# Two graph layers on one NeuronCore: first-layer sums one turn behind their messages, no shared PSUM banks, whole pair buffers in the second layer, and SyncE register loads without an assert

## The chip, the core and the metric

The kernel runs on one core of one Trainium2 chip. The metric is the device time of one execution in microseconds (us). Engines are written as the profile writes them: PE is TensorE (PEld its weight loads), DVE VectorE, ACT ScalarE, POOL GpSimd, SP SyncE (SPq is its queue of DMA issues). PEclk is the clock that TensorE was granted, in tenths of full speed.

## What is computed

There are 6,250 nodes with 512 features and 100,000 edges, sorted by destination. Destinations are drawn as the square of a uniform number, so low-numbered nodes have more incoming edges.

```python
def gat(feat, dist, src, dst, W, b, w_src, w_dst):          # layer 0
    h = leaky_relu(feat @ W.T + b, 0.2).reshape(N, 8, 64)
    e = leaky_relu((h * w_src).sum(-1)[src] + (h * w_dst).sum(-1)[dst], 0.2)
    m = segment_max(e, dst)
    ex = exp(e - m[dst])
    s = segment_sum(ex, dst)
    msg = h[src] * (ex / s[dst] * dist)[:, :, None]
    return segment_sum(msg, dst).reshape(N, 512)

def sage(x, src, dst, deg, W_self, W_neigh, bias, gamma, beta):   # layer 1
    h = x @ W_self.T + (segment_sum(x[src], dst) / deg) @ W_neigh.T + bias
    return layernorm(h) * gamma + beta

x = x + gat(relu(layernorm(x)), edge_attr_8, ...)
x = x + sage(relu(layernorm(x)), ...)
```

All is float32.

## The kernel before

**Streams, windows, turns.** The sorted edge list is cut into four streams q of equal length. Streams 0 and 1 are pair 0, streams 2 and 3 pair 1. Each stream is walked in NW = 66 windows of T = 3 tiles of 128 edges. A window of a stream touches at most 64 destination rows, starting at a base row that is looked up in a table; windows of stream 0 share one base in groups of four, those of stream 1 in groups of two, and streams 2 and 3 change it each window (GRP = (4, 2, 1, 1)). One pass through the loop body is a turn.

**First layer, node part.** The first 265 us hold the layer norm and the dense product of layer 0; the results go to a table `h0_d` in DRAM, each row with the 512 values of h and the 8 of e_src. `ed_d` holds e_dst.

**First edge loop** (about 265 to 1450 us). For each window POOL fetches the h rows of 12 tiles, one indirect DMA each (`gather`, L731), into one of NB = 4 window buffers `gbuf`. `load_edges` has SP fetch the destination rows' e_dst (L766) and the segment penalties (L768). `onehot` (L774, DVE) makes the 0/1 matrices of edge to destination; they are turned over on PE (`front_turn`, L793) and multiplied with e_dst (`front_dst`, L805). `soft_pick` (step ECa, ACT, L822) picks e_src out of the gathered rows and `soft_src` (SSa, PE, L814) adds it to the same bank. Scans on DVE find the maximum of each segment (NX, SCF, SCR), PE turns the result (TE, TM, L860), LM/SUB/EXP/AA make the weights, and the messages are formed in place in `gbuf`: D0c to D1b on DVE (L954, L961), the H steps on ACT (L973). Then the sums: `add_ones` (SV, L998) and the six `add_up` steps A00 to A12 (L990) multiply the one-hot matrices with the messages into one PSUM bank per pair. `finish` (C0, C1) adds the window before, moved to the new base by a selector matrix CS (`carry_sel`), with an f32 matmul (L1007, and L1008 for the weight sums). `evac` (EV0, EV1, L1018) copies the bank to SBUF tile `ws` on ACT; `store` has SP write rows whose base is done. Finished blocks of 128 nodes ("slots") are loaded back by `slot_load`, divided, added to x, normalised and written to `h1_d` by `slot_run`, a generator that ORDER advances at each "S" and "L".

**What sets the order.** Nothing is reordered by a scheduler: the program runs under a manual schedule, so each engine's queue follows the order in which Python calls the steps. ORDER is that list for a turn k; STEPS gives for each name the window it works on, as an offset from k. FT0=(4, …) works on window k+4, A00=(0, …) on window k. `when` drops steps outside 0 to 65. At the end of a turn the twelve gathers of window k+4 are issued; each waits until the sum that last read its part of the buffer is done.

**Shared banks.** `goes_on(k, p)` is true for pair 0 at odd windows, where neither stream 0 nor stream 1 changes its base. There the bank is not evacuated after window k-1 and not carried: the matmuls of window k go on adding to it. In layer 0 this starts at window KR = 9, since up to there the carried sum may have to be rescaled; in layer 1 at window 1.

**Second edge loop** (about 1590 to 2650 us). The same streams and windows without attention: POOL gathers 12 tiles of `h1_d` per turn (`gather1`, L1273) into a ring of five buffers of half a window each; PE sums (L1302); the carry is split in two parts (`carry_split`, L1333 and L1334, DVE) and added with two fp32r matmuls (`finish1`, L1310); ACT evacuates (L1322). In the same turns each finished slot goes through the dense products (L581), the layer norm and the residual. ORDER1 and STEPS1 lay out this turn.

**SP's register loads.** `base` and `slot_load` read a row number from SBUF into a register (L721 and others). In the trace each is a TENSOR_LOAD, a FUSED_REGOPS and a SEQ_ASSERT on SP.

Of the kernel before, what the change touches and what calls it, by code (L numbers as in the profile page):

```python
# [8 lines left out]
FT = mybir.dt.float32  # L9
FR = mybir.dt.float32r  # L10
# [34 lines left out]
def gnn_kernel(ctx, tc, x, srcp, dstp, attrp, wt0, b0, wsrc, wdst, wts, wtn, bias1, gamma1, beta1, out):  # L45
# [3 lines left out]
    order.enter_context(tc.manual_schedule())  # L49

# [144 lines left out]
    btab = con.tile([1, NQ, NW], I32, name="btab")  # L195
# [149 lines left out]
    def i_base():  # L345
        V.tensor_copy(dfr, dstt[0:1, :, 0:NL:T])
        V.tensor_scalar(bmx, bhi[0:1, :], -float(M), 0.0, op0=OP.add, op1=OP.max)
        V.tensor_tensor(out=br, in0=dfr, in1=bmx.unsqueeze(2).to_broadcast([1, NQ, NW]), op=OP.min)
        V.memset(br[:, 0, 0:1], 0.0)
        for q in range(NQ):  # L350
            for i in range(1, GRP[q]):
                n = len(range(i, NW, GRP[q]))
                V.tensor_copy(br[:, q, i::GRP[q]], br[:, q, 0:NW:GRP[q]][:, 0:n])
        V.tensor_copy(btab, br)
        yield
        yield
# [361 lines left out]
    def base(k, q):  # L718
        k -= k % GRP[q]
        if (k, q) not in breg:  # L720
            breg[k, q] = S.value_load(btab[0:1, q, k:k + 1], min_val=0, max_val=N - M)  # L721
        return breg[k, q]
# [11 lines left out]
    def attr_turn(k, h):  # L734

        c, kk = divmod(k, CH)
        if kk == CH - 3 + h // 4 and (k < 0 or (c + 1) * CH < NW):
            c += 1
            nt = min(CH * T, NL - c * CH * T)
            if h == 0:  # L740
                AT[c] = lp.tile([128, H, NQ * CH * T], FT, name="at")
                AT.pop(c - 2, None)
            av = AN[c].rearrange("t (e h) -> t h e", h=H)
            AP_[h] = pv = bank("sf"[(k - 1) % 2])[:, 0:4 * NQ * nt].rearrange("p (h t) -> p h t", h=4)
            for i in range(4):
                P.transpose(pv[:, i], av[0:NQ * nt, h + i], ident[0:NQ * nt, 0:NQ * nt])
            if h:
                AN.pop(c)
# [176 lines left out]
    def fac_rest(k):  # L925
        F9[k] = f9 = lp.tile([128, 2, H + 2], FT, name="f9")
        V.tensor_scalar(f9[:, :, H + 1], FP[k][:, :, H], -1.0, 1.0, op0=OP.mult, op1=OP.add)
# [47 lines left out]
    BANKS = [bank("w", 2) for _ in range(2)]  # L975

    def goes_on(k, p, first=KR):

        return p == 0 and first <= k < NW and k % GRP[0] and k % GRP[1]

    def add_up(k, p, j):
        if j >= njof(k):
            return
        oh, g_ = OHs[k], GT[k]
        if j == 0:
            BK[p] = BANKS[p]
        w = BK[p]
        for q2 in range(2):
            r = slice(64 * q2, 64 * q2 + 64)
            P.matmul(w[r, :], oh[:, p, j, q2], g_[:, 2 * p + q2, j, 0:D], start=(j == 0 and not goes_on(k, p)), stop=False, skip_group_check=True)  # L990
# [10 lines left out]
    def finish(k, p):  # L1001

        w, sv = BK.pop(p), SV[k]
        if k:
            c = WC[k] if k < KR else WS[k - 1]
            if not goes_on(k, p):
                P.matmul(w, CS[k][:, p], c[:, p, 0:D], start=False, stop=True, skip_group_check=True)  # L1007
            P.matmul(sv[:, p], CS[k][:, p], c[:, p, None, D:AW].to_broadcast([128, 2, H + 1]), start=False, stop=True, skip_group_check=True)  # L1008
        BK[k, p] = w
        if p:  # L1010
            GT.pop(k)

    def evac(k, p):
# [3 lines left out]
        if not goes_on(k + 1, p):  # L1017
            A.activation(WS[k][:, p, 0:D], w, AF.Copy)  # L1018
# [10 lines left out]
    def store(k, p, acc, width):  # L1029
        for q2 in range(2):  # L1030
# [8 lines left out]
            if k + 5 < NW:  # L1039
                base(k + 5, q)  # L1040
# [11 lines left out]
    def slot_load(s, r=None):  # L1052
        if r is None:
            r = S.value_load(tab[0:1, s:s + 1], min_val=0, max_val=NP - 128)
# [40 lines left out]
    def none():  # L1095
        return iter(())
# [3 lines left out]
    10 01 00 30 11 20 02 22 12 21 31 32  # L1100
# [4 lines left out]
    for k in range(NB - 1):  # L1105
        gather(k)
# [19 lines left out]
    def slot(w):  # L1126
# [8 lines left out]
        FT0=(4, front_turn, 0), FT0c=(4, front_copy, 0), FT1=(3, front_turn, 1), FT1c=(3, front_copy, 1),  # L1135
        FD=(3, front_dst), ECa=(3, soft_pick, 0), SSa=(3, soft_src, 0), ECb=(2, soft_pick, 1), SSb=(2, soft_src, 1), EZ=(2, soft_copy), SCF=(2, max_before), NX=(2, max_ahead),
# [4 lines left out]
        RESC=(0, later(rescale, KR)), D0c=(0, message_part), D0a=(0, message, 0, 0), D0b=(0, message, 0, 1), D1a=(0, message, 1, 0),  # L1141
        D1b=(0, message, 1, 1),
        SV=(0, add_ones), A00=(0, add_up, 0, 0), A01=(0, add_up, 0, 1), A02=(0, add_up, 0, 2),
        A10=(0, add_up, 1, 0), A11=(0, add_up, 1, 1), A12=(0, add_up, 1, 2), C0=(0, finish, 0), C1=(0, finish, 1),
        EV0=(0, evac0), EV1=(-1, evac1), OH=(4, onehot), CS=(0, later(carry_sel)))
    STEPS.update({f"H{p}{i}": (0, message_act, p, i) for p in range(2) for i in range(4) if p or i})
    ORDER = """
    H13 H01 D0b S D0a D1a TE ECb H11 NX S SCR S FT1 A00 D0c FL EV1 SV S H12 RESC A01 AT0 H03 H02 OH TM A10 S CM FDf A02
    FX S RS S LM RH AT0c CS SSb C0 SUB PF L FT1c S EZ EXP D1b SCF S A11 H10 AT1 ECa AT1c FT0 S AA F9a S A12 F9b S EV0
    FD SSa C1 FT0c S  # L1150
# [9 lines left out]
    for k in range(-4, NW + 1):  # L1160
        sl_ = slot_run(slot(k - 3)) if slot(k - 3) is not None and slot(k - 3) not in LATE else none()
        c, kk = divmod(k, CH)
        when(k + 4, load_edges)
        if slot(k - 2) is not None and slot(k - 2) not in LATE:
            slot_load(slot(k - 2))
# [16 lines left out]
        if k >= -1:  # L1182
            when(k + NB, gather)
# [84 lines left out]
    def gather1(k, p):  # L1268
        GT[k, p] = g_ = ring[:, (2 * k + p) % 5]
        for j in range(njof(k)):  # L1270
            for q2 in (1, 0):
                c = k * T + j
                G.indirect_dma_start(out=g_[:, q2, j, :], out_offset=None, in_=h1_d[0:NT * 128, :],  # L1273
                                     in_offset=bass.IndirectOffsetOnAxis(ap=idx[:, 2 * p + q2, c:c + 1], axis=0))
# [3 lines left out]
    ring = lay1.enter_context(tc.tile_pool(name="gp1", bufs=1)).tile([128, 5, 2, T, D], FT, name="g")  # L1278
    own1 = wp1.tile([128, LATES, D], FT, name="own1")
    small = lay1.enter_context(tc.tile_pool(name="small1", bufs=5))  # L1280
    with tc.tile_pool(name="raw1", bufs=1) as tmp:
# [5 lines left out]
        for n in range(5):  # L1287
            gather1(*divmod(n, 2))
# [6 lines left out]

    def add_up1(k, p, j):
        if j >= njof(k):
            return
        if j == 0 and not goes_on(k, p, 1):
            BK[p] = bank("w", 2) if p else bank("s")  # L1300
        for q2 in range(2):
            P.matmul(BK[p][64 * q2:64 * q2 + 64, :], OHs[k][:, p, j, q2], GT[k, p][:, q2, j, :],  # L1302
                     start=(j == 0 and not goes_on(k, p, 1)),
                     stop=False, skip_group_check=True)

    def finish1(k, p):
        w = BK[p]
        if k and not goes_on(k, p, 1):
# [8 lines left out]
    def evac1_(k, p):  # L1317
        if p == 0:
            WS[k] = lp.tile([128, 2, D], FT, name="ws")
        w = BK.pop((k, p))  # L1320
        if not goes_on(k + 1, p, 1):
            A.activation(WS[k][:, p], w, AF.Copy)  # L1322
# [4 lines left out]
    def carry_split(k, p):  # L1327

        if goes_on(k + 1, p, 1):
            return  # L1330
# [6 lines left out]
    def slot1_load(s, r=None):  # L1337
        if r is None:
            r = S.value_load(tab[0:1, s:s + 1], min_val=0, max_val=NP - 128)
# [9 lines left out]
    def own_load(s):  # L1349
        r = S.value_load(tab[0:1, s:s + 1], min_val=0, max_val=NP - 128)  # L1350
# [116 lines left out]
    PIECES = [ring[:, (2 * NW + i // (2 * T)) % 5, i % (2 * T) // T, i % T] for i in range(NLATE)]  # L1467

    def late_sums(i):
        s = LATE[i]  # L1470
        y = PIECES[i]
# [68 lines left out]
    def early(w, f):  # L1540
        return at(w, f) if slot(w) not in LATE else none()

    STEPS1 = dict(EV0=(0, evac1_, 0), CS0=(-1, carry_split, 0), EV1=(-1, evac1_, 1), CS1=(-1, carry_split, 1), OH=(1, onehot, 3),
                  SEL=(1, carry_sel, FR), C0=(0, finish1, 0), C1=(0, finish1, 1), G0=(3, gather1, 0), G1=(2, gather1, 1))
    STEPS1.update({f"A{p}{j}": (0, add_up1, p, j) for p in range(2) for j in range(T)})
    SLOTS1 = dict(MEAN=(-2, slot1_mean), SUMS=(-1, slot1_sums))
    ORDER1 = """
    en en la MEAN A00 A01 A02 la A10 CS0 C0 EV1 OH en PUT en PRE G1 sl la SEL en en SUMS CS1 sl A11 A12 EV0 G0 C1 sl  # L1550
    """.split()

    last, ends = none(), none()
    for k in range(-1, NW - 1):
# [5 lines left out]
        for name in ORDER1:  # L1560
            if name == "sl":
                step(sl_)
            elif name == "la":
                step(last)
            elif name == "en":
                step(ends)
            elif name == "PUT":
                run(ends)
                put_out()
            elif name == "PRE":  # L1570
                run(pre)
            elif name in SLOTS1:
                d, f = SLOTS1[name]
                early(k + d, f)
            elif k >= 0 or name[0] != "G":
                d, f, *a = STEPS1[name]
                when(k + d, f, *a)
        if 12 <= k < 12 + NLATE:
            late_beta(k - 12)
        last, ends = sl_, last  # L1580
    k = NW - 1
    sl_ = early(k - 2, slot1_run)
    carry_split(k - 1, 0)
# [188 lines left out]
```

## Time and profile before

Three runs took 2757.96, 2762.36 and 2772.39 us, the median being 2762.36.

| | profiled execution |
|---|---|
| its own time | 2755.29 us |
| span in the trace | 2753.4 us |
| mean granted PE clock | 0.866 |
| PE busy | 2154.7 us (78%) |
| POOL busy | 1699.9 us (62%) |
| DVE busy | 1524.9 us (55%) |
| ACT busy | 1106.5 us (40%) |
| gathers, layer 0 | 784, mean 973 ns on POOL |
| gathers, layer 1 | 784, mean 978 ns on POOL |

The 1.9 us between span and time lie outside the traced span. The page divides the span into 40 slices of 69 us. In slices 5 to 21 (the first edge loop) DVE and ACT show 4 to 7 tenths, in slices 24 to 38 (the second) 4 to 5 and 1 to 2, while PE shows 8 in nearly all. A share over the whole span mixes these stages, so the stages are read one by one: by busy times in windows of the span, by what ended each idle time of an engine, and by the chain of waits that ended last.

### The profile page before, as it was taken

The page shows a single profiled execution, that of the slowest core. Times are in us where ns is not written, and L with a number is a line of the kernel's source. Part 1 is how long each engine was busy: PE and PEld are TensorE (multiplying, and loading weights), DVE is VectorE, ACT ScalarE, POOL GpSimd, SP SyncE. Part 2 cuts the span into 40 slices and gives each one's busy share as a digit, 9 for nine tenths or more (in the row PEclk, how much of TensorE's full clock was granted, in tenths as well). Part 3 has the DMA queues.
Part 4 walks back from the last instruction along what each step waited for, and adds up shares of the span by engine and source line. Part 5 has one row for each costly group of instructions (what it writes and reads, how often), then busy time and mean ns, then how long its engine had stood idle before and what let it go on. Part 6 is the DMA issues. An engine that isn't in the chain of part 4 may idle for free.

```text
span 2753.4 us, 34180 instructions
## 1 busy us (share of the span) xinstructions
PE 2154.7 (78%) x8780; PEld 1068.8 (39%) x8780; DVE 1524.9 (55%) x3120; ACT 1106.5 (40%) x3469; POOL 1699.9 (62%) x1675
## 2 busy tenths in 40 slices
PE   7982688888888888888885266787887788878886
PEld 5761233333333333333332033343443444434444
DVE  7874556576667666666667122254544444444446
ACT  6860445566556565555654111122222222222212
POOL 5666466666666666666652666666667666766652
PEclk9995789888888998898987588898898898998898
DMA  6636476777787888877774777788878787878872
GB/s 206 203 114 181 129 205 191 218 239 230 235 246 237 240 236 238 241 237 235 241 221 129 244 214 221 235 250 251 254 240 257 237 258 243 251 248 249 252 238 91
DMA packets 264713, 611.63 MB, mean 222 GB/s; under 512 B 63604, under 2 KB 74372, under 8 KB 264510
## 3 DMA queue, kind: packets, MB, share of 16 engines
q0 software_dynamic: 125440, 414.35, 51.6%
q1 hardware_dynamic: 138494, 193.97, 21.3%
q8 instruction: 72, 1.18, 0.2%
q14 instruction: 131, 1.07, 0.1%
q10 hardware_dynamic: 576, 1.05, 0.1%
HBM read 511.44 MB, written 97.76 MB: 221 GB/s over the span
## 4 chain that ended last, share of the span: by engine, by line
PE 50%; issue 16%; DVE 15%; another core or an unknown queue 9%; ACT 5%; DMA 3%; POOL 1%; SPq 1%; ACTq 0%; POOLq 0%; DVEq 0%
PE ps_w L990 10%; PE ps_b L581 6%; PE ps_s L1302 6%; PE ps_f L581 5%; PE ps_w L1302 5%; DVE gbuf L954 3%; PE ps_z L805 2%; PE ps_w L1007 2%; ACT gbuf L973 2%; PE ps_w L1310 2%; PE ps_t L793 1%; PE ps_w L581 1%; PE ps_s L998 1%; PE ps_z L814 1%
## 5 line engine op out<-in xcount | busy, mean ns | idle before, releaser
L731 POOL DMA_INDIRECT gbuf<-h_d,idx x784 | 762.6, 973 | 461.3 <-issue 197.7
L1273 POOL DMA_INDIRECT g<-h_d,idx x784 | 766.9, 978 | 391.0 <-issue 198.8
L990 PE MATMUL ps_w<-gbuf,oh 128*64 128x512 f32 x1568 | 524.8, 709 | 79.1 <-issue 47.4
L973 ACT ACTIVATE gbuf<-gbuf,aa 128x64 f32<-128x64 f32 x1788 | 452.0, 334 | 4.5 <-issue 2.3
L954 DVE TENSOR_TENSOR gbuf<-gbuf,ps_c 128x1024 f32<-128x1024 f32 x260 | 308.3, 1214 | 0.5 <-issue 0.5
L1302 PE MATMUL ps_w<-g,oh 128*64 128x512 f32 x784 | 220.8, 637 | 18.8 <-issue 15.1
L1302 PE MATMUL ps_s<-g,oh 128*64 128x512 f32 x784 | 189.5, 618 | 49.2 <-issue 45.4
L1400 ACT ACTIVATE hs<-sx,slc 128x512 f32<-128x512 f32 x45 | 36.6, 814 | 366.7 <-remote 110.3
L990 PEld LDWEIGHTS ps_w<-gbuf,oh 128*64 128x64 f32 x1568 | 105.7, 150 | 201.5 <-issue 135.8
L841 DVE TENSOR_TENSOR_SCAN nx<-penb,ms,ps_z 32x256 f32<-32x256 f32 x66 | 48.1, 728 | 235.9 <-remote 149.3
L617 POOL TENSOR_TENSOR pr<-hr,watt 128x1024 f32<-128x1024 f32 x47 | 113.1, 2411 | 76.0 <-DVE hr L614 69.4
L797 ACT ACTIVATE oht<-ps_t 128x384 f32<-128x384 f32 x132 | 63.8, 483 | 199.1 <-issue 56.8
L1389 DVE TENSOR_TENSOR lo<-ps_t,hi 128x512 fp32r<-128x512 f32 x55 | 37.9, 688 | 184.7 <-issue 84.9
L1018 ACT ACTIVATE ws<-ps_w 128x512 f32<-128x512 f32 x103 | 60.0, 582 | 176.3 <-remote 81.6
L774 DVE TENSOR_TENSOR oh<-ps_c,dsr 128x768 f32<-128x768 f32 x130 | 123.1, 947 | 1.1 <-DVE ps_c L704 1.1
L1322 ACT ACTIVATE ws<-ps_w 128x512 f32<-128x512 f32 x66 | 39.2, 594 | 192.2 <-remote 62.5
L793 PE MATMUL ps_t<-ident,oh 128*128 128x128 f32 x392 | 79.9, 318 | 40.1 <-DVE oh L774 27.2
L581 PE MATMUL ps_f<-ws_whi,hi 128*128 128x512 f32 x112 | 55.1, 492 | 71.5 <-issue 47.5
L805 PE MATMUL ps_z<-oht,edb 128*32 128x384 f32 (+1 forms) x264 | 109.7, 543 | 1.3 <-DVE mf L834 1.3
L1302 PEld LDWEIGHTS ps_s<-g,oh 128*64 128x64 f32 x784 | 51.5, 139 | 152.2 <-issue 143.1
L1310 PE MATMUL ps_w<-chi,cs 128*128 128x512 f32 x65 | 37.3, 575 | 91.5 <-issue 71.1
L1007 PE MATMUL ps_w<-ws,cs 128*128 128x512 f32 x170 | 98.4, 661 | 11.3 <-DVE et L872 6.0
(397 smaller groups left out, 3996.2 us busy)
## 6 DMA issues: line engine op xcount, KB each, us to landing
sx<-x SPq DMA_DIRECT2D x95, 256.0 KB
acc_d<-ws SPq DMA_DIRECT2D x182, 130.2 KB
acc_d<-ws SPq DMA_DIRECT2D x182, 128.0 KB
h_d<-hr SPq DMA_DIRECT2D x49, 260.0 KB
gbuf<-h_d,idx POOLq DMA_INDIRECT x784
g<-h_d,idx POOLq DMA_INDIRECT x784
sa<-acc_d SPq DMA_DIRECT2D x48, 260.5 KB
s<-acc_d SPq DMA_DIRECT2D x48, 256.0 KB
```

What stands on the lines that cost most here:

```text
L581: P.matmul(pt, a_[:, k], w_[:, k], start=not last[0], stop=stop and k == 3 and w_ is whi_ and a_ is lo)
L617: G.tensor_tensor(out=pr, in0=hr[:, None, 0:D].to_broadcast([128, 2, D]), in1=watt, op=OP.mult)
L731: G.indirect_dma_start(out=g_[:, q, j, :], out_offset=None, in_=h0_d, in_offset=bass.IndirectOffsetOnAxis(ap=idx[:, q, c:c + 1], axis=0))
L774: V.tensor_tensor(out=oh.rearrange("p a j b n -> p (a j b) n"), in0=c_iota[:, None, :].to_broadcast([128, 4 * T, M]), in1=dsr[:, k].rearra ...
L793: P.transpose(pt[:, j * 128:j * 128 + 128], OHs[k][:, p, j].rearrange("e b n -> e (b n)"), ident)
L805: P.matmul(z[0:NQ * H, 0:n], ed_tile(k, p), oht[:, p, 0:n], start=(p == 0), stop=False, skip_group_check=True)
L954: eng.tensor_tensor(out=x4, in0=x4, in1=(AA if eng is V else A2)[k][:, i, q].unsqueeze(3).to_broadcast([128, 2, H, D // H]), op=OP.mult)
L973: A.activation(x_, x_, AF.Copy, scale=A2[k][:, T - 1, 2 * p + q2, h:h + 1])
L990: P.matmul(w[r, :], oh[:, p, j, q2], g_[:, 2 * p + q2, j, 0:D], start=(j == 0 and not goes_on(k, p)), stop=False, skip_group_check=True)
L1007: P.matmul(w, CS[k][:, p], c[:, p, 0:D], start=False, stop=True, skip_group_check=True)
L1273: G.indirect_dma_start(out=g_[:, q2, j, :], out_offset=None, in_=h1_d[0:NT * 128, :], in_offset=bass.IndirectOffsetOnAxis(ap=idx[:, 2 * p ...
L1302: P.matmul(BK[p][64 * q2:64 * q2 + 64, :], OHs[k][:, p, j, q2], GT[k, p][:, q2, j, :], start=(j == 0 and not goes_on(k, p, 1)), stop=False ...
```

## The change

1. **First edge loop: the sums run one turn later.** SV, all A and C steps, EV0, CS and RESC work on window k-1 in turn k (offset -1 where it was 0), EV1 on k-2. The messages stay at window k. The loop has one turn more; slots are loaded and finished one turn later. The gather at the end of turn k is that of window k+3 (it was k+4), and four windows are gathered ahead of the loop (it was three).
2. **e_src is picked later.** ECa and SSa work on window k+2 (it was k+3), but early in the turn, not near its end. OH and FT0 work on k+3 (it was k+4). ORDER and TILES, the order of a window's twelve gathers, are new.
3. **No shared banks.** `goes_on` is gone: every window starts its bank anew, is carried and evacuated, in both layers. In layer 0 the banks rotate through `bank("w", 2)`, in layer 1 through three.
4. **Second layer.** The ring of five half-window buffers, with dependencies by piece, becomes a pool of five whole buffers: the first gather into one waits for the last sum that read it. `gather1` takes a whole window, k+3, at the end of the turn. The turn is written out by calls in place of ORDER1: pair 0's evacuation is at the start of the next turn, not at the end of its own, and `slot1_pre` (PRE) runs near the end.
5. **SP's loads.** Register loads have no assert; `load_both` reads the two bases of a pair in one load, for which `btab` is laid out by window. Bases are loaded six windows ahead (it was five).

```diff
+    def load_both(at, most):
+        return nc.values_load_multi_w_load_instructions(
+            at, engines=(mybir.EngineType.SP,), min_val=0, max_val=most,
+            skip_runtime_bounds_check_because="VectorE has clamped the table to this range")[1]
...
     def base(k, q):
+        p = q // 2
         k -= k % GRP[q]
-        if (k, q) not in breg:
-            breg[k, q] = S.value_load(btab[0:1, q, k:k + 1], min_val=0, max_val=N - M)
-        return breg[k, q]
+        if (k, p) not in breg:
+            breg[k, p] = load_both(btab[0:1, k, 2 * p:2 * p + 2], N - M)
+        return breg[k, p][q % 2]
...
         if j == 0:
-            BK[p] = BANKS[p]
+            BK[p] = bank("w", 2)
...
-            P.matmul(w[r, :], oh[:, p, j, q2], g_[:, 2 * p + q2, j, 0:D], start=(j == 0 and not goes_on(k, p)), stop=False, skip_group_check=True)
+            P.matmul(w[r, :], oh[:, p, j, q2], g_[:, 2 * p + q2, j, 0:D], start=(j == 0), stop=False, skip_group_check=True)
...
-            if not goes_on(k, p):
-                P.matmul(w, CS[k][:, p], c[:, p, 0:D], start=False, stop=True, skip_group_check=True)
+            P.matmul(w, CS[k][:, p], c[:, p, 0:D], start=False, stop=True, skip_group_check=True)
...
-        if not goes_on(k + 1, p):
-            A.activation(WS[k][:, p, 0:D], w, AF.Copy)
+        A.activation(WS[k][:, p, 0:D], w, AF.Copy)
...
     TILES = [(int(t[0]), int(t[1])) for t in """
-    10 01 00 30 11 20 02 22 12 21 31 32
+    00 20 10 21 31 01 30 02 22 32 11 12
-    for k in range(NB - 1):
+    for k in range(NB):
         gather(k)
...
     ORDER = """
-    H13 H01 D0b S D0a D1a TE ECb H11 NX S SCR S FT1 A00 D0c FL EV1 SV S H12 RESC A01 AT0 H03 H02 OH TM A10 S CM FDf A02
-    FX S RS S LM RH AT0c CS SSb C0 SUB PF L FT1c S EZ EXP D1b SCF S A11 H10 AT1 ECa AT1c FT0 S AA F9a S A12 F9b S EV0
-    FD SSa C1 FT0c S
+    EV1 D1b H13 SV A00 S A10 OH H02 A01 D0c D0a ECa RS RESC S H01 SSa CS ECb A11 NX S H12 SCR H03 S S TE A02 S C0 SSb
+    TM H10 FL D0b FT0 FDf EV0 S FT0c S CM D1a A12 EZ LM FX S RH L SUB FT1 S SCF PF EXP AA S C1 AT0 FT1c AT0c S AT1 AT1c
+    F9a H11 F9b FD
     """.split()
...
-    for k in range(-4, NW + 1):
+    for k in range(-4, NW + 2):
...
-        if k >= -1:
-            when(k + NB, gather)
+        if k >= 1:
+            when(k + NB - 1, gather)
...
-    def gather1(k, p):
-        GT[k, p] = g_ = ring[:, (2 * k + p) % 5]
-        for j in range(njof(k)):
-            for q2 in (1, 0):
+    def gather1(k):
+        for p in range(2):
+            GT[k, p] = g_ = g1.tile([128, 2, T, D], FT, name="g")
+            for j in range(njof(k)):
+                for q2 in range(2):
...
-    ring = lay1.enter_context(tc.tile_pool(name="gp1", bufs=1)).tile([128, 5, 2, T, D], FT, name="g")
+    g1 = lay1.enter_context(tc.tile_pool(name="gp1", bufs=5))
...
+    def bank_s():
+        s_[0] = (s_[0] + 1) % 3
+        return bank("s") if s_[0] == 0 else bank("w", 2)
...
-    ORDER1 = """
-    en en la MEAN A00 A01 A02 la A10 CS0 C0 EV1 OH en PUT en PRE G1 sl la SEL en en SUMS CS1 sl A11 A12 EV0 G0 C1 sl
-    """.split()
...
+        when(k - 1, evac1_, 0)
+        early(k - 2, slot1_mean)
+        step(sl_)
+        when(k, add_up1, 0, 0)
+        step(ends)
+        when(k - 1, carry_split, 0)
...
+        when(k, add_up1, 0, 2)
+        step(ends)
+        when(k, finish1, 0)
+        step(sl_)
+        run(ends)
+        put_out()
+        when(k - 1, evac1_, 1)
+        early(k - 1, slot1_sums)
+        when(k, add_up1, 1, 0)
+        when(k - 1, carry_split, 1)
+        when(k + 1, carry_sel, FR)
+        when(k, add_up1, 1, 1)
+        when(k, add_up1, 1, 2)
+        step(sl_)
+        run(pre)
+        when(k, finish1, 1)
+        step(last)
...
+        if k >= 0:
+            when(k + 3, gather1)
```

## The prediction

> **What bounds the kernel now.** The page first: no engine is busy all the time and DMA is busy at 0.8, so the sum of the span says little. I went to the windows of the two edge loops, which hold 2,245 of 2,753 us.
>
> ```profile
> 600.00:1400.00 800.00, 684.99 (x2874) 290.32 (x2874) 528.99 (x1061) 476.50 (x1813) 508.08 (x525) 0.88 0.80 237
> 1700.00:2600.00 900.00, 721.74 (x2767) 369.23 (x2766) 404.40 (x870) 195.69 (x370) 596.80 (x609) 0.89 0.80 248
> ```
>
> Columns: window, length, busy us (count) of PE, PEld, DVE, ACT, POOL, then granted clock, DMA share, GB/s. POOL's count gives the pace: 525 gathers by 12 are 43.75 turns in 800 us, 18.3 us each; 609 by 12 are 50.75 in 900, 17.7 us each. A layer-0 turn holds 15.7 us of PE, 12.1 of DVE, 10.9 of ACT. POOL seems free, but each gather brings 0.30 us of issue beside its 0.97:
>
> ```profile
> POOL gbuf L731 <- issue: 133.2, 424, 3.1
> POOL gbuf L731 <- PE ps_w L990: 49.7, 31, 3.0
> POOL gbuf L731 <- PE ps_z L814: 32.8, 22, 2.2
> POOL gbuf L731 <- PE ps_z L805: 27.8, 17, 2.2
> ```
>
> (Waits of POOL in 600 to 1400: total, times, longest.) 12 × (0.95 + 0.30) = 15.0 us is POOL's floor for a turn. The three lower rows are 110 us, 2.5 us a turn, in which POOL waits on PE: for buffers that A and SSa still read. So PE sets the pace by when it frees buffers, and POOL is close behind. What PE waits for, same window:
>
> ```profile
> PE ps_w L990 <- issue: 39.6, 38, 2.3
> PE ps_f L1008 <- DVE et L872: 17.0, 13, 2.0
> PE ps_w L990 <- DVE gbuf L954: 14.4, 16, 0.9
> PE ps_w L1007 <- DVE et L872: 3.7, 2, 3.0
> PE ps_w L990 <- ACT gbuf L973: 2.5, 3, 1.6
> ```
>
> Rows 2 and 4 are C0 waiting for CS, which stands behind LM (L872) on DVE; rows 3 and 5 are sums waiting for messages formed in the same turn. That is 37.6 us, 0.86 a turn. Row 1 has no cause in the profile. Lastly the timeline:
>
> ```profile
> 936.42 0.74 DVE L841 TENSOR_TENSOR_SCAN nx<-penb,ms,ps_z 32x256 f32<-32x256 f32 x1 [8.30 <-remote]
> 936.46 0.60 ACT L1018 ACTIVATE ws<-ps_w 128x512 f32<-128x512 f32 x1 [7.65 <-remote]
> ```
>
> DVE and ACT stood 8 us and then went on at one instant. Starts of OH (L774) lie alternately about 24 and 12.6 us apart: such a freeze begins every second turn. PE work that they wait for was issued long before, so its signals come late; in the same stretch three of SP's edb loads (L766) take 4.72 us, against 0.47 for the median one. The chain of waits has five pieces of 8.3 to 9.0 us in 600 to 1400 under "another core or an unknown queue". I don't know the cause.
>
> **The change, first loop.** *Removed:* the 0.86 us above. With sums a turn behind messages, A's inputs are old when PE gets there; CS and the window before's evacuation are early too. The half clock goes with the gaps: 34 half-speed spells, 184 us, lie in 600 to 1400. Here a rule and the rows differ. The Trainium skill (TensorE: Matmul & The Clock Gate, "The HAM clock gate") has the clock fall after an idle window of about 3.4 us. By that, gaps of at most 3 us, as in the rows above, cost no clock, and closing them returns 0.86. By the trace, half-speed spells come in steps of 3.413 us as the page says, but 34 times, many after gaps of 1 to 2 us. If a third of the 184 us goes, and half-speed matmuls take twice as long, 30 us of PE time return, 0.7 a turn. I take the row: 0.86 + 0.7 = 1.56.
>
> *Added:* 29 carries (odd windows 9 to 65), two L1007 records each, laid back to back 1.13 us: 33 us, or 0.57 a turn over 57 turns; this is PE, the bound. 29 evacuations at 0.58 us are 17 us of ACT, which is busy 10.9 of 18.3: nothing. So 1.0 us net a turn. Check from below: laid end to end from warm records (A six pairs at 1.0, C 2.3 with its small part, SV 1.5, FD 1.3, FT 1.0, SSa and SSb 0.9, TE and TM 0.7), PE needs about 13.7 us, so POOL's 15.0 plus its usual 0.8 of unhidden waits is the next stop, 15.8. The estimate, 18.3 − 1.0 = 17.3, lies between. Times 62 full turns: **−62** us.
>
> *ECa and SSa moved* to the front of the turn. Queued behind ECa on ACT: RESC's input, H01 and EV0; behind SSa on PE: CS-dependent C0 and all later A. Both now need window k+2, whose last gather was issued at the end of turn k−1: the buffer was freed by A11 or A12 of that turn. The ring is A11 → seven gathers (8.75) → landing → ECa 0.25 → SSa 0.55 → A11 1.0. Landing by the packet records is 4.2 us (3.5 to 4.9) from POOL's start, so 14.8 us. The Trainium skill (DMA: Bandwidth & Descriptors, "Anatomy of one DMA") gives 2.0 us plus bytes over 436e3; for 266,240 bytes that is 2.6 and a ring of 13.2. By the rule 4.1 us are spare in a turn of 17.3; by the row 2.5. I use the row: just hidden, price 0. In before, ECa lay at the turn's end, some 10 us later, so that cover is gone: where landing takes 2.5 us more, PE waits.
>
> *One more turn* with no gathers drains sums: a turn's A and C, about 9 us, less the shorter ramp (e_src a window nearer, one gather more ahead): **+5**.
>
> **Second loop.** 33 carries (odd 1 to 65) of two fp32r matmuls, 0.56 us a pair: 18 us of PE; 33 evacuations at 0.59 us = 19 of ACT; 33 × (0.46 + 0.71) = 38 of DVE, which is busy 8.0 of 17.7. DVE and ACT hide theirs. PE is busy 14.2 of 17.7:
>
> ```profile
> PE ps_w L1310 <- issue: 66.2, 30, 9.7
> PE ps_f L581 <- issue: 33.3, 17, 12.0
> ```
>
> PE's idle before the carry is large, and splitting each window makes a carry out of turns that had none, each waiting for evacuation and split (0.59 + 1.17 us). The lower end is 0 (it falls into the 3.5 us of idle a turn), the upper 33 × (0.56 + 1.76) = 77. Nearest is the first row, idle at carries of 2.2 us each, but issued after work that overlaps: I take 18. *Whole buffers:* the first gather into a buffer waits for the last of six sums, not for the first, about 3 us later; POOL has 17.7 − 15.0 = 2.7 a turn and the pair is wanted over a turn later: 0 to +20 over the loop, I take 5. *Written-out order:* PRE late covers slot loads longer (DVE waits 53.6 us for acc_d there), pair 0's evacuation early delays nothing that C0 needs sooner; −20 to +30, I take +2. Sum **+25**.
>
> **SP.** 121 loads of 0.32, 0.21 and 0.135 us lie in 600 to 1400, but SPq is 1% of the chain, so the shorter program is worth 0, unless it is what freezes the others. Also bases come two by one load. From −150 to 0.
>
> **Sum:** −62 + 5 + 25 = −32 against the 2755.29 of the profiled execution: 2723. The median of the runs shown is 7 us above that execution, so I state 2730; the rivals' times stand to the median as well.
>
> **Rivals.**
> *A. Late e_src (slower).* For it: the new cover is 2.5 us, and gathers do land late inside freezes of 8 us; POOL and SP share DMA at 0.80. Each freeze in every second turn would then expose landing (4.2 us): 2.1 a turn, × 62 = +130; −62 + 30 of the forecast's own sum leave +98: 2860. It decides from landings over about 6.7 us. Against: the freeze also holds PE, whose later A's would wait anyhow.
> *B. PE is the bound and clock doesn't recover (slower).* −0.86 + 0.57 = −0.29 a turn = −18, +5, second loop at +50, nearer the upper end of its carries: +37, 2799.
> *C. The asserts made the freezes.* For it: SP slow in just those stretches, and the second turn, with four base loads, has them; against: the edb DMAs stay, and the chain names SP at 1%. If half of each 8 us goes, 33 × 4 = 132 more: 2598.
> *D. The change moves waits, not the pace:* DMA at 0.80 and POOL at 15.0 of 18.3 hold; 2760.
>
> **Numbers.** Forecast 0.38 (own range 2670 to 2748), A 0.19, B 0.22, C 0.11, D 0.10. Differences within 0.5% (14 us) can't be told from no change by these runs. Faster: 0.38 + C = 0.49; same: D = 0.10; slower: A + B = 0.41. The range leaves out half of C and the far part of A: 2600 to 2840.
>
> **What would show it.** Right: the layer-0 pace at 17.3 us per 12 gathers, rows "L1008 <- DVE et" and "L990 <- gbuf" gone, granted clock above 0.88, L1007's count up by 58, L1310's by 66. Wrong: PE waiting at L814 on gathers or ACT es (A); PE busy up with clock 0.88 (B); starts of OH evenly apart and no 8 us pieces (C). A second-loop pace above 18.2 would overthrow the +25.

## The result and the profile after

The changed kernel takes 2876.82 us (median of 4 runs, 2871.22 to 2885.45), the kernel before 2761.46 beside it: ratio 1.0395, 95% interval 1.0371 to 1.0420. It is slower by 115 us; 2730 with a range of 2600 to 2840 was forecast. The profiled execution has a span of 2869.4 us at a mean clock of 0.858.

The windows view of the kernel after, with the columns of the prediction's first fence (window, length, busy us and count of PE, PEld, DVE, ACT, POOL, granted clock, DMA share, GB/s):

```profile
600.00:1400.00 800.00, 624.05 (x2637) 282.01 (x2637) 475.18 (x956) 443.62 (x1659) 464.93 (x475) 0.84 0.74 215
1700.00:2600.00 900.00, 751.45 (x2769) 354.16 (x2770) 403.97 (x856) 199.41 (x372) 594.19 (x606) 0.91 0.78 243
```

475 gathers by 12 are 39.6 turns in 800 us, 20.2 us a turn against 18.3. The second loop has 50.5 turns in 900, 17.8 against 17.7. So +1.9 × 62 = +118 us: the whole loss lies in the first loop. PE is busy for 15.8 us of a turn there, as before (15.7), and its idle time rose from 2.6 to 4.4: PE is not busier, it waits. For what, in the waits view of PE in 600 to 1400 of the kernel after (total us, times, longest; `issue` means that the profile shows nothing that was waited for, `remote` a sender that it can't name):

```profile
PE ps_t L805 <- ACT oht L809: 86.8, 18, 6.2
PE ps_z L817 <- issue: 36.8, 21, 5.6
PE ps_t L805 <- issue: 24.0, 11, 5.3
PE ps_z L826 <- ACT es L834: 15.2, 7, 4.3
```

The rows that the change was to remove, C0 waiting for CS and sums waiting for messages, are gone. In their place PE stands before FT1 (L805), whose bank FT0c on ACT (L809) has to empty first. POOL, same window:

```profile
POOL gbuf L743 <- PE ps_w L996: 136.4, 48, 7.8
POOL gbuf L743 <- issue: 111.7, 354, 2.8
POOL gbuf L743 <- ACT s_y L191: 35.1, 15, 2.7
```

POOL's waits for the sums (L996, L990 before) went from 49.7 us, longest 3.0, to 136.4, longest 7.8. One such stretch in the timeline of the kernel after (start, length, engine, line, idle before and its end):

```profile
855.75 0.55 PE L805 MATMUL ps_t<-ident,oh 128*128 128x128 f32 x3
...
858.99 0.95 POOL L743 DMA_INDIRECT gbuf<-h_d,idx  x1 [0.30 <-issue]
...
861.47 0.49 ACT L809 ACTIVATE oht<-ps_t 128x384 f32<-128x384 f32 x1 [4.51 <-remote]
...
862.02 0.90 PE L805 MATMUL ps_t<-ident,oh 128*128 128x128 f32 x3 [4.71 <-ACT oht L809]
```

FT0's transposes are over by 856.4, but ACT, with nothing else to do, starts their copy at 861.47. PE's signal came 5 us late, and now PE itself hangs on it through FT1. That is the stall of the prediction's timeline, now in a place where PE can't run on. The first row of PE's waits above has 18 such waits in some 40 turns.

**What ends a stall.** For POOL's gaps between gathers I took all over 0.6 us (600 ns, twice the usual 0.30) in 550 to 1100 us of each trace, and call them pauses. A stall is a gap of over 2.5 us in PE's signals (the semaphore updates that the trace records) that ends with at least three of them, each within 60 ns of the one before.

```
                          pauses a turn   mean us   together   turn us
kernel before                 1.93          1.88       3.63     18.3
kernel after                  1.82          3.06       5.58     20.4
```

15.0 us of gathers and the pauses together make the turn in both, within 0.4 us. In the first sixteen stalls after 600 us of the kernel before, PE's signals came 1.26 to 2.53 us after POOL's last gather had ended, in those of the kernel after 1.14 to 2.42 us. And of the 434 PE signals recorded in 550 to 1100 us of the kernel before, 269 came 2 to 4 us after a gather began, in a pause. This suggests that PE's signals are held while POOL issues gathers back to back. It doesn't prove it: POOL pauses because it waits for such a signal, so a pause must end with one.

SP gives a sign that doesn't hang on POOL's pauses, for no wait of POOL's is put down to SP. In 300 to 1250 us of the kernel before, 324 of some 2,060 SP instructions began 0.68 to 0.75 us after the one before. By POOL's state these are 12 of 511 in the first 2 us of a run of gathers (less than 0.6 us apart), 249 of 1,095 later in a run, 63 of 412 in the 2.5 us after it, and none of 47 later still. So something slows SP when POOL has issued gathers for some 2 us, and this ends soon after; whether it is the issuing or the traffic of these gathers, this can't say. Before the first gather, at 224 us, the trace has no stall and records all of PE's 104 signals; in 600 to 1250 us it records 497 of 644.

The number of stalls doesn't follow the time, though: in 300 to 1250 us there are 33 in the kernel before and 26 in the kernel after, and of the runs below the slow a_front has 4 and the faster a_pause 40. What follows the time is the sum of POOL's pauses (4.6 us a turn in a_again, 8.3 in a_front, 10.4 in b_three), as it must where twelve gathers take 15.0 us of a turn. It says where the time goes, not why.

### The profile page after: what moved, and what is told of

Same layout as the page of the kernel before. It is cut to its first block, busy times and chain, and to the rows that moved or that the text cites. A ratio compares the mean times of both kernels' runs of the same rounds, so it can differ in the third digit from the quotient of the medians.

```text
span 2869.4 us, 33051 instructions
## 1 busy us (share of the span) xinstructions
PE 2223.2 (77%) x8904; PEld 1093.8 (38%) x8904; DVE 1552.3 (54%) x3186; ACT 1146.2 (40%) x3531; POOL 1708.5 (60%) x1675
## 4 chain that ended last, share of the span: by engine, by line
PE 57%; issue 15%; DVE 7%; another core or an unknown queue 6%; ACT 5%; POOL 5%; DMA 4%; ACTq 0%; SPq 0%; DVEq 0%; POOLq 0%
PE ps_w L996 12%; PE ps_w L1314 8%; PE ps_w L1012 5%; POOL g L1278 4%; PE ps_f L592 4%; PE ps_z L817 4%; PE ps_b L592 4%; PE ps_s L1314 4%; PE ps_t L805 2%; PE ps_s L1004 2%; ACT gbuf L985 2%; PE ps_z L826 2%; DMA g<-h_d,idx 2%; PE ps_w L1321 2%
## 5 line engine op out<-in xcount | busy, mean ns | idle before, releaser
L996 PE MATMUL ps_w<-gbuf,oh 128*64 128x512 f32 x1568 | 431.1, 661 | 0.4 <-issue 0.4
L1314 PE MATMUL ps_w<-g,oh 128*64 128x512 f32 x1048 | 325.2, 642 | 117.1 <-issue 62.2
L805 PE MATMUL ps_t<-ident,oh 128*128 128x128 f32 x392 | 85.8, 336 | 193.2 <-ACT oht L809 131.6
L1314 PE MATMUL ps_s<-g,oh 128*64 128x512 f32 x520 | 163.7, 662 | 34.4 <-issue 31.0
L817 PE MATMUL ps_z<-oht,edb 128*32 128x384 f32 (+1 forms) x264 | 146.7, 684 | 54.2 <-issue 47.7
L1314 PEld LDWEIGHTS ps_w<-g,oh 128*64 128x64 f32 x1048 | 77.4, 141 | 268.9 <-issue 244.6
L809 ACT ACTIVATE oht<-ps_t 128x384 f32<-128x384 f32 x132 | 63.3, 480 | 282.0 <-remote 177.6
L1340 DVE CAST chi<-ws 128x512 fp32r<-128x512 f32 x130 | 56.3, 433 | 177.5 <-ACT ws L1331 99.5
L1396 DVE TENSOR_TENSOR lo<-ps_z,hi 128x512 fp32r<-128x512 f32 x48 | 33.1, 689 | 220.1 <-issue 181.4
L1012 PE MATMUL ps_w<-ws,cs 128*128 128x512 f32 x228 | 150.2, 746 | 0.0
L996 PEld LDWEIGHTS ps_w<-gbuf,oh 128*64 128x64 f32 x1568 | 96.5, 146 | 125.9 <-issue 113.3
L805 PEld LDWEIGHTS ps_t<-ident,oh 128*128 128x128 f32 x392 | 48.0, 162 | 252.2 <-ACT oht L809 159.5
L1395 ACT ACTIVATE hi<-ps_z 128x512 fp32r<-128x512 f32 x48 | 28.7, 597 | 259.1 <-remote 104.7
```

The source lines that it names most:

```text
L805: P.transpose(pt[:, j * 128:j * 128 + 128], OHs[k][:, p, j].rearrange("e b n -> e (b n)"), ident)
L817: P.matmul(z[0:NQ * H, 0:n], ed_tile(k, p), oht[:, p, 0:n], start=(p == 0), stop=False, skip_group_check=True)
```

## The experiments

Each ratio is to the kernel before beside it on the same chip. The runs went to five chips, and these differ: on one, that of the runs whose names begin with e, the kernel before takes 2387 us and no trace has such a stall; on the other four it takes 2740 to 2762 us, and every trace has some. I call the first quiet. The changed kernel itself was not run there, and on the others its ratio lies between 1.0287 and 1.0395, so a difference of a point between two chips says nothing.

| run | ratio | 95% interval | chip |
|---|---|---|---|
| e1_loads | 1.0007 | 0.9998 to 1.0017 | quiet |
| e2_unshared | 1.0007 | 0.9994 to 1.0019 | quiet |
| e3_second | 0.9972 | 0.9960 to 0.9983 | quiet |
| e5_turn_early | 1.0381 | 1.0359 to 1.0403 | quiet |
| b_second_loads | 0.9928 | 0.9902 to 0.9955 | stalls |
| a_again | 1.0287 | 1.0243 to 1.0332 | stalls |
| a_tiles | 1.0618 | 1.0553 to 1.0683 | stalls |
| a_swap | 1.0441 | 1.0389 to 1.0493 | stalls |
| f_plain | 1.0354 | 1.0304 to 1.0403 | stalls |
| f_tiles | 1.0683 | 1.0662 to 1.0705 | stalls |
| f_turn | 1.0377 | 1.0348 to 1.0406 | stalls |
| f_tiles_turn | 1.0746 | 1.0700 to 1.0792 | stalls |
| b_pick_later | 1.0070 | 1.0045 to 1.0094 | stalls |
| b_three | 1.1319 | 1.1283 to 1.1355 | stalls |
| a_front | 1.1134 | 1.1104 to 1.1164 | stalls |
| b_pause | 1.0176 | 1.0153 to 1.0198 | stalls |
| a_front_pause | 1.0772 | 1.0742 to 1.0801 | stalls |
| a_pause | 1.0158 | 1.0117 to 1.0199 | stalls |

### The parts alone

Register loads alone: the diff of `load`, `load_both`, `base` and `btab` above, on the kernel before.

> The kernel before with SP's register loads of the change alone (no assert, both bases of a pair in one load, six windows ahead). Theory F (the turn's new order costs all of the loss, SP nothing): 2755 to 2770 us, stalls of about 8 us in every second turn as before. Theory S (SP's dense programs cause the stalls): 2600 to 2700 us, stalls half as long. Theory S reversed (loads without assert let SP run ahead and disturb more): above 2790 us.

1.0007: nothing. As that chip has no stalls, this can't say whether the loads make them; b_second_loads below can.

Shared banks away in the first loop alone:

```diff
-        return p == 0 and first <= k < NW and k % GRP[0] and k % GRP[1]
+        return first == 1 and p == 0 and first <= k < NW and k % GRP[0] and k % GRP[1]
```

> The kernel before with the shared banks taken from the first loop alone: 29 more carries and evacuations. Theory F: the carries cost their PE time at most, 33 us, so 2775 to 2800 us. Theory B (shared banks are what the loss is made of: without them every turn waits for its carry): 2830 us or more, a first-loop turn of 19.5 us or more. If PE's idle time takes the carries in: 2762 to 2772 us.

1.0007, that is, not to be told from nothing. PE's busy time rose, but not the turn. The windows view, first of e1_loads, which has the first loop of before, then of e2_unshared:

```profile
500.00:1100.00 600.00, 557.60 (x2591) 245.47 (x2590) 476.29 (x953) 427.09 (x1629) 456.56 (x471) 0.97 0.91 285
```

```profile
500.00:1100.00 600.00, 573.18 (x2606) 255.47 (x2605) 476.66 (x953) 430.59 (x1624) 455.45 (x468) 0.95 0.91 284
```

471 and 468 gathers in 600 us: a turn of 15.3 and 15.4. On the quiet chip POOL's 15.0 set the pace, and 16 us more of PE fitted into PE's idle time. On a chip with stalls the carries were not tried alone.

The second loop alone, with its gathers, order and banks as in the diff above, on the kernel before:

> The kernel before with the second loop of the change alone (whole buffers, written-out order, no shared banks there). Theory F: the second loop's pace is nearly unchanged (17.8 against 17.7 us a turn), 2755 to 2785 us. Forecast on record: +25, 2787 us. A second loop that costs half of the loss: 2815 us or more.

0.9972: 7 us faster. Second loop and loads together, on a chip with stalls:

> The kernel before with the change's second loop and its register loads together; the first loop stays as it was. If the parts add up: 0.997 to 0.998 of the kernel before (second loop alone 0.9972, loads alone 1.0007). With that the whole of the loss lies in the first loop. If loads and second loop disturb one another: 1.005 or more.

0.9928, better than both kernels. Its trace still has the stalls (31 in 300 to 1250 us, where that of before has 33), so the asserts don't make them. And only the first loop of the change is left to lose.

### FT0 and FT1

FT0 and FT0c half a turn ahead of FT1, in the changed kernel:

```diff
-    EV1 D1b ... ECb A11 NX S H12 SCR ... D0b FT0 FDf EV0 S FT0c S CM ...
+    EV1 D1b ... ECb A11 NX S FT0 H12 FT0c SCR ... D0b FDf EV0 S S CM ...
```

> The changed kernel with two steps moved: the first transposes FT0 go right behind A11 and their copy FT0c right behind H12, half a turn ahead of FT1, which needs the same bank. Theory F (PE stands before FT1 because FT0c has to come through ACT first, 2.8 us a turn in the trace): the first-loop turn falls from 20.2 to 17.5 to 18.3 us, total 2755 to 2800 us. Rival M (the stall comes from outside and only moves to the next cross-engine wait): 2850 to 2890 us, with PE waiting somewhere else for as long.

On the quiet chip it loses too, 1.0381. With the first loop of before (e1_loads) POOL doesn't pause there at all in 550 to 1100 us, and here it does, 1.9 us a turn. The waits of e5_turn_early in 500 to 1100 us, of ACT, PE and POOL:

```profile
ACT es L834 <- DMA gbuf<-h_d,idx: 102.1, 35, 5.9
```

```profile
PE ps_z L826 <- ACT es L834: 78.5, 34, 4.5
```

```profile
POOL gbuf L743 <- PE ps_w L996: 66.3, 56, 3.6
```

The same rows in e1_loads (its lines are numbered otherwise):

```profile
ACT es L834 <- DMA gbuf<-h_d,idx: 78.2, 23, 7.5
PE ps_z L826 <- ACT es L834: 33.0, 24, 4.4
POOL gbuf L743 <- PE ps_w L1002: 5.8, 19, 0.3
```

ACT waits for gathers in both; what is new is how long PE waits for ACT and POOL for PE. This fits the ring that the prediction named: the gather lands, ECa picks e_src, SSa and the sums behind it on PE follow, they free the buffer for the next gather. 423 gathers in 600 us are a turn of 17.0, against 15.3. It is read from the trace alone: the edits that shorten the ring ran only on chips with stalls.

On those, a square of four runs: the changed kernel (f_plain), another tile order (f_tiles), FT0 early (f_turn), both (f_tiles_turn). The first two were also run on another chip (a_again, a_tiles). The tile order:

```diff
-    00 20 10 21 31 01 30 02 22 32 11 12
+    00 20 10 30 01 11 21 31 02 12 22 32
```

> The changed kernel itself beside the kernel before on the chip of the experiments, for its trace and its ratio there. Both theories: 1.035 to 1.045 of the kernel before; a first-loop turn near 17 us against 15.3. Theory R (ring: the gathers of a window are issued behind A11 and wanted by ECa early in the next turn) expects ACT to stand before ECa for DMA, and PE before SSa for ECa.

> The changed kernel with another order of a window's twelve gathers: the eight that ECa reads (j 0 and 1) first, the four of j 2 last, so that ECa waits for the eighth and not the eleventh. Theory R: three gathers of 1.25 us less in the ring, so the first-loop turn falls from 17.0 to 15.3 to 15.7 us and the total by 75 to 105 us, to 0.99 to 1.01 of the kernel before. Rival P (PE's own work with the carries, or the transposes, sets the turn): less than 30 us gained, 1.025 or more.

> The changed kernel unaltered, as the base of a square of four (tile order changed or not, FT0 moved or not) on one chip. On a chip without the stalls of PE's signals (kernel before near 2387 us): 1.035 to 1.045, ACT standing before ECa for DMA. On a chip with them (kernel before 2740 to 2762 us): 1.028 to 1.040 as measured twice.

> The square's second corner: the eight gathers that ECa reads first, the four of j 2 last. Theory R (the ring of gather, landing, ECa, SSa, A11) on a chip without stalls: 75 to 105 us less than the changed kernel, 0.99 to 1.01 of the kernel before. On a chip with stalls the order lost 97 us to the changed kernel (1.0618 against 1.0287); the same again would show that the ring doesn't set the turn there.

> The square's third corner: FT0 and its copy FT0c half a turn earlier. On a chip without stalls: within 15 us of the changed kernel (1.038 was measured beside 1.035 to 1.045 expected). On a chip with stalls theory F (PE stands before FT1 for FT0c, through ACT, while its own signals are late): 60 to 120 us less than the changed kernel; rival M (the stall moves to the next wait between engines): within 20 us of it.

> The square's fourth corner, both edits. Theory R with nothing else in the way, on a chip without stalls: as f_tiles, 0.99 to 1.01. If tile order helps only where FT0 is early: f_tiles at 1.03 and this at 1.00. On a chip with stalls theory F: 60 us or more below f_tiles.

FT0 early: 1.0377 against 1.0354, nothing gained. PE's waits in 600 to 1300 us, first of f_plain, then the largest of f_turn:

```profile
PE ps_t L805 <- issue: 36.0, 16, 5.7
PE ps_t L805 <- ACT oht L809: 20.5, 4, 5.7
```

```profile
PE ps_z L817 <- issue: 73.0, 23, 6.7
PE ps_z L817 <- DVE mf L846: 36.5, 7, 6.4
```

The waits before FT1 (L805; 86.8 and 24.0 us in the first trace) are gone, and PE stops at the next wait between engines, FD (L817): all waits of PE together are 145 us in f_plain and 153 in f_turn. So they were not the cause, and theory F fell. The tile order lost 3.3 points both times (1.0618 and 1.0287, 1.0683 and 1.0354), and 3.7 with FT0 early (1.0746 and 1.0377). The ring of theory R, under which it should have gained, doesn't set the turn on these chips; why the order loses so much stays open. A11 ahead of SSa lost as well:

```diff
-    ... ECa RS RESC S H01 SSa CS ECb A11 NX ...
+    ... ECa RS RESC S H01 A11 SSa CS ECb NX ...
```

> The changed kernel with A11 ahead of SSa on PE, not behind it; nothing else is moved. Theory R: A11 and the gathers that it releases no longer wait for the e_src of the gathers before, so POOL's waits for PE fall and the turn by 0.8 to 1.5 us: 50 to 90 us gained, ratio 1.00 to 1.02. Rival P: within 10 us of the changed kernel.

1.0441 against 1.0287: the buffer is free earlier, and the kernel slower.

### Slack of the buffers

In the kernel before, ECa and SSa alone moved to the next turn's start, first with four buffers, then with three:

```diff
-        FD=(3, front_dst), ECa=(3, soft_pick, 0), SSa=(3, soft_src, 0), ...
+        FD=(3, front_dst), ECa=(2, soft_pick, 0), SSa=(2, soft_src, 0), ...
-    H13 H01 D0b S D0a D1a TE ECb ...
+    H13 H01 D0b S D0a D1a TE ECa SSa ECb ...
```

```diff
-NB = 4
+NB = 3
```

> The kernel before with ECa and SSa alone moved: from the end of turn k (window k+3) to the start of turn k+1, as the change has it; sums, shared banks, four buffers stay. Control of the next run. Theory K (slack: what costs is that a buffer is held a turn longer while its refill is wanted at nearly the same time): 0.99 to 1.01 of the kernel before, since the refill has a turn to spare. Rival O (the new place of e_src is itself the cost): 1.025 to 1.045.

> The run above with three window buffers in place of four: a buffer is refilled one turn nearer to ECa, the distance that the lagging sums leave in the changed kernel, without lag, added carries, new ORDER or transposes. Theory K: 1.03 to 1.07 of the kernel before, POOL standing before L731 for sums 4 us or more a turn. Rival P (carries and order): 0.99 to 1.015.

1.0070 and 1.1319. The place of e_src by itself costs 0.7%; a turn of slack less, at that place, costs 12 points more, with no lag, no added carry and no new order. The waits of b_three in 600 to 1300 us:

```profile
POOL gbuf L731 <- PE ps_w L990: 267.0, 65, 7.1
ACT es L822 <- DMA gbuf<-h_d,idx: 141.1, 46, 7.5
PE ps_z L814 <- ACT es L822: 147.8, 22, 8.3
```

It lost far more than the change, and more than theory K had allowed (1.07). Here A12, which frees the last of the buffer, stands at the end of the turn, in the changed kernel nearer its middle, so the slack is smaller here. That lost slack can cost this much is shown; how much of the change's loss it is, is not. The lag alone, with the old order, was not run.

### Late signals

All six sums of the old window at the front of the turn, in the changed kernel:

```diff
-    EV1 D1b H13 SV A00 S A10 OH H02 A01 D0c ... ECb A11 NX ... TE A02 S ... D1a A12 EZ ...
+    EV1 D1b H13 SV A00 S A10 OH H02 A01 A11 A02 A12 D0c ... ECb NX ... TE S ... D1a EZ ...
```

> The changed kernel with A11, A02 and A12 moved up behind A01, ahead of SSa: all six sums of the last window at the start of the turn, so that its buffer is free about 6 us earlier. Theory K: 50 to 110 us less than the changed kernel (1.03 to 1.04), so 0.99 to 1.02. Rival P: 1.03 or more. A11 alone ahead of SSa gave 1.044 on a chip with stalls, which speaks for P there.

1.1134: far slower, against theory K: the buffer is free earlier, and that gains nothing. The POOL rows of its timeline show what it does:

```profile
703.05 0.94 POOL L743 DMA_INDIRECT gbuf<-h_d,idx  x1 [6.14 <-PE ps_w L996]
704.29 0.95 POOL L743 DMA_INDIRECT gbuf<-h_d,idx  x1 [0.30 <-issue]
...
717.50 0.94 POOL L743 DMA_INDIRECT gbuf<-h_d,idx  x1 [0.30 <-issue]
727.84 0.95 POOL L743 DMA_INDIRECT gbuf<-h_d,idx  x1 [9.39 <-PE ps_w L996]
```

Twelve gathers in a row without a stop, then 9.4 us of nothing, then the next twelve. The other engines have waits as long, for PE or for a sender that the profile can't name (DVE's in 600 to 1300 us):

```profile
DVE nx L853 <- PE ps_w L1012: 48.0, 6, 8.7
DVE nx L853 <- remote: 47.6, 4, 14.2
```

If PE's signals are held while POOL issues (theory H), the work that needs a hand-over between engines has to wait for POOL's pause, and the turn becomes POOL's run plus that work. This can be tested with work added to POOL: in a_front eight memsets of 128x128 (207 ns each) after the third, sixth and ninth gather of a window.

```diff
+            if n_ in (3, 6, 9) and k >= NB:
+                for _ in range(8):
+                    G.memset(idle, 0.0)
```

> The run with all sums at the front (a_front, 1.1134), with about 1.9 us of small memsets on POOL after the third, the sixth and the ninth gather of a window: 5.7 us more work on POOL in each turn. Theory H (on a chip with stalls, PE's signals are held while POOL issues gathers back to back; a_front lets it issue ten in a row): faster by 60 to 150 us although POOL has more to do, 1.06 to 1.09, first-loop turn 20.5 to 22 us against 22.9. Rival (the order itself, or late signals of another origin): slower or the same, 1.11 to 1.24. On a chip without stalls: POOL 20.7 us a turn, 1.13 to 1.15 in both.

1.0772 against 1.1134. POOL has 768 memsets, 159 us, more to do in these 700 us, and the kernel is about 3.6 points faster. The two ran on different chips, but the changed kernel differs by 1.1 points between chips, not by 3.6. POOL's waits in 600 to 1300 us, of a_front and then with the pauses:

```profile
POOL gbuf L743 <- PE ps_w L996: 241.4, 39, 12.3
```

```profile
POOL gbuf L747 <- issue: 102.1, 331, 1.3
POOL gbuf L747 <- PE ps_w L1000: 14.8, 25, 3.1
```

The wait for sums fell from 241.4 us to 14.8, and the granted TensorE clock didn't help (0.77 in this window against 0.79). DVE's waits before NX did not fall:

```profile
DVE nx L857 <- issue: 187.6, 21, 11.3
DVE nx L857 <- PE ps_z L830: 103.2, 10, 12.4
```

So POOL no longer stands still for the sums, but the hand-overs between the other engines still take their time. The same with one pause, after the sixth gather, in the changed kernel and in the kernel before:

> The changed kernel with one such pause of 1.9 us after the sixth gather of a window. Theory H: POOL's long waits for PE shrink by most of what the pause costs, 1.02 to 1.05. Rival: the 1.9 us come on top, 62 turns of them 118 us, 1.07 to 1.085. On a chip without stalls: 1.04 to 1.06 in both.

> The kernel before with eight small memsets (about 2 us together) put on POOL between the sixth and the seventh gather of a window. Theory H (on chips where PE's signals come late, they are held while POOL issues gathers back to back and pass when it pauses): there the pause takes the place of a forced one, 0.975 to 1.01. Rival (signals late for another reason): 1.02 to 1.045. On a chip without stalls, where POOL sets the turn: 1.045 to 1.055 in both.

The changed kernel goes to 1.0158, from 1.0287 to 1.0395 without the pause on other chips: about two fifths to three fifths of the loss is given back by adding 1.9 us of work to each turn. In the kernel before the pause costs 1.8%, 49 us, where 62 turns of the 2.3 us that it takes there would be 141. That is more than the 1% that theory H had allowed and just under its rival's 2%: about two thirds are hidden, which the 3.6 us that POOL stands still in each turn could hide without theory H. So the two runs that became faster speak for it, and this one decides nothing. The reading is that POOL's breaks let PE's signals through; that they merely spread the transfers was not tried apart, and no pause was tried on the quiet chip.

## Why the prediction was wrong

- **The step that failed is the one from PE's waits to the turn.** The rows to be removed were named rightly and are gone, but the 1.0 us a turn did not follow: the sum rests on "So PE sets the pace by when it frees buffers, and POOL is close behind" and on "POOL's 15.0 plus its usual 0.8 of unhidden waits is the next stop, 15.8". POOL's 15.0 and its pauses already made up the turn, and the pauses were 3.6 us a turn, not 0.8; the prediction's own rows have 2.5 of waits for PE. The change took the pauses to 5.6, and that is its +1.9 us a turn. The new order of the turn was priced at nothing in these terms: the five stalls of over 8 us were seen, their cause put down as unknown, and the sum left them as they were. Why the pauses grew is shown in part. Work added to POOL gives back about half the loss, carries and loads cost nothing where they were tried alone, and which of lag, place of e_src and order makes the rest stays open.
- **"Just hidden, price 0"** for ECa and SSa: too low. Their place alone costs 0.7% (b_pick_later), and with a turn less between the freeing of a buffer and the use of its refill 13% (b_three). That this is what the lag costs is not shown: the edits that free the buffer earlier (a_swap, a_front) lost. On the quiet chip e5_turn_early has a turn of 17.0 against 15.3, with PE waiting for ECa. On the chip of the result late landing isn't it: L826 waits 15.2 us for ECa in 800, and of 475 gathers, with a median of 3.6 us from POOL's start to the last data packet, none took over 6.7, the time from which rival A would count. So rival A came near the measured time (2860 forecast, 2876.82 measured) by luck.
- **The clock:** by the row I expected 0.7 us a turn back; the clock went from 0.88 to 0.84, and the half-speed spells in 600 to 1400 us from 184 us to 253. PE's gaps over 3.4 us went from 1 to 25. In the kernel before there were 34 spells beside that one gap, which the rule doesn't explain; with 37 spells and 25 gaps in the kernel after, the trace no longer tells rule and row apart.
- **Carries**, 33 us on PE: their price on the quiet chip is nothing that can be measured (e2_unshared). Rival B, PE as the bound, falls there; on the chip of the result PE's busy time a turn stayed at 15.8 us, so its mechanism isn't seen there either.
- **Second loop, +25:** its sign was wrong: 7 us gained on the quiet chip (e3_second), about 19 on one with stalls, together with the loads (b_second_loads). 17.8 against 17.7 us a turn on the chip of the result was well within the 18.2 that I had named as the bound.
- **SP, 0:** right (e1_loads). Rival C, that asserts make the stalls, falls by b_second_loads, which has none and stalls all the same. But "three of SP's edb loads (L766) take 4.72 us, against 0.47" was a misreading: the 4.72 run from the start of the first to the end of the third, which take 0.70, 0.50 and 0.47 us. The time went into the register load between them. Rival D falls with the result.
- **The extra turn, +5**, was not measured by itself.

## What to carry to other kernels

Moving a consumer one step behind its producer keeps every buffer in between a step longer: count when the buffer is freed and when its refill is wanted before counting the waits that go. Engines' waits in a profile can change places without changing the pace, so before an edit is priced by the row it removes, ask which engine's pauses fill the turn, and take the sum of its work and pauses as the thing to explain. Try an edit on more than one chip: here the same kernel differs by 15% between them, and an order tuned for one limit meets another.

## What the runs showed of the hardware

- One kernel, the one before, takes 2387 us on one chip and 2740 to 2762 on four others. The difference goes with stalls of PE's signals: none in the traces of the first by the test above, 33 in 300 to 1250 us of the first trace shown here. On the quiet chip the trace records 764 of PE's 766 signals in 600 to 1250 us (e1_loads), in that first trace 497 of 644.
- On those chips adding work to POOL between gathers made two kernels faster (1.1134 to 1.0772; 1.0287 to 1.0395 down to 1.0158), each pair measured on different chips. Whether it is the breaks in the issuing or the spread of the transfers is not shown.
- In the same stretches SP is slow too: the two instructions of one register load take 0.71 us each within a stall (at 933.47 and 934.18 us in the kernel before), and 0.28 and 0.15 us right after it (at 937.52 and 937.85). Steps of 0.68 to 0.75 us make up 324 of some 2,060 in 300 to 1250 us of the kernel before, and 4 of 2,496 in e2_unshared on the quiet chip, with the same SP program for its loads.
